# A message-passing layer on one core: relative destinations read from one SBUF partition, in place of memory, and whole loads in place of queued parts

## The chip, the cores and the metric

The kernel runs on one core of one Trainium2 chip. Its time is device microseconds of one execution; the number given for a kernel is the median over its runs. Engines are named as in the profile: PE (TensorE), DVE (VectorE), ACT (ScalarE), POOL (GpSimd) and SP (SyncE, which here only issues DMAs). SBUF is the on-chip memory with 128 partitions, HBM the large memory outside.

## The reference

A graph has 6250 nodes with 128 features each and 100000 edges, sorted by destination. For every edge the features of its source node, of its destination node and of the edge itself go through one linear layer, a layer norm and a ReLU. The messages are summed by source node, added to the nodes, and layer-normed again.

```python
def _L0_gnn_ref(x, edge_index, edge_attr, W, b, gamma, beta):
    row, col = (edge_index[0], edge_index[1])          # src, dst
    msg_in = jnp.concatenate([x[row], x[col], edge_attr], axis=-1)
    h = msg_in @ W + b
    mu = jnp.mean(h, axis=-1, keepdims=True)
    var = jnp.mean(jnp.square(h - mu), axis=-1, keepdims=True)
    h = (h - mu) * jax.lax.rsqrt(var + LN_EPS) * gamma + beta
    msg = jax.nn.relu(h)
    return jax.ops.segment_sum(msg, row, num_segments=x.shape[0])

x = _layernorm(x + _L0_gnn_ref(x, stack([src, dst]), edge_attr_128, ...), axis=-1)
```

## The kernel before, in words

The edges are cut into 782 tiles of 128 edges. Four tiles make a piece; there are 196 pieces, and the main loop runs one piece per slot. Piece numbers are q in the code. Five splits of the tiles (164, 168, 168, 164 and 118) are handled one after another: while the pieces of one split go through the first stage, the pairs of node blocks of the split before go through the second.

First stage, for a piece q. `edge_loads` (L471) brings in eT, the transposed edge features (128 features x 1024 edges, float32, two pieces), and db (128 partitions x 1024, bfloat16), which holds in every partition the same row: for each of the 1024 edges the destination relative to the first destination of its piece. `edge_window` (L506) loads win, the 42 rows of the projected node table that the piece's destinations lie in, three bfloat16 parts one above the other (126 partitions). `edge_hot` (L518) compares db with the partition's number on DVE (L528) and so makes the one-hot matrix ohd. `edges` (L531) multiplies on PE: eT with its part of the weights (L540) and ohd with win (L544), both into the PSUM tile hp. `scatters` (L548) copies hp to one of eight hs buffers on ACT (L552, L553), and POOL writes each tile's 128 rows with an indirect DMA (L557) to their places in the table `sorted` in HBM, where the edges of a block of source nodes lie together. Pieces 0 and 1 (`BY_PE = 2`) don't use db: PE repeats their row.

Second stage, for a pair of node blocks: `load_pair` (L600, DMA at L604) brings its rows of `sorted` back as hl (four buffers), and the class `Pair` adds the source node's projection, norms, applies the ReLU and sums by node, over PE, ACT and DVE. `clear` (L191) fills the unused places of `sorted` from an SBUF tile of 48 partitions that holds empty rows. The last split's pairs form the tail, with no first stage beside them.

Where the relative destinations come from: `windows` (L264) computes on DVE the tile drel, 98 partitions x 2 x 512, bfloat16. One partition holds the rows of two pieces, 2 KB. When its second half is done, POOL stores drel to the HBM tensor drel_d (L271), and every db load reads its row of drel_d 128 times (step 0 over the partitions of db).

The loads of eT and db: up to q = 8 (`FROM = 9`) one DMA each for two pieces (for q = 0 one for each piece), and for piece 2 db's load is on POOL's queue. From q = 10 on `edge_loads` issues nothing itself; it appends six parts to the list `parts`: four DMAs of eT with 32 partitions each, and after the second and the fourth of them one DMA of db with 64 partitions. `part_loads` (L502, DMA at L504) issues the next one on SP. It is called three times a slot: before `edge_hot`, before `scatters`, and at the slot's end, so that the six parts go out over two slots.

The order of PE, DVE, ACT and SP is written out by hand (`manual_schedule`): each engine does its instructions in the order in which the code issues them. A slot q of the main loop (L901 to L931) calls in this order: steps of the node projections (first split), `edge_loads` and `edge_window` up to four pieces ahead, `clear_pairs`, `part_loads(1)`, `edge_hot(q + 2)`, `edges(q)`, one step of `work` (the second stage, which also issues the hl loads), `part_loads(1)`, `scatters(q)`, steps of `places`, the rest of `work`, `part_loads(1)`. SP waits in this order too: a DMA whose buffer is not free holds up those behind it. eT and db have three buffers of two pieces each, win six.

Of the kernel before, what the change touches and what calls it, by code (L numbers as in the profile page):

```python
# [9 lines left out]
BF16 = mybir.dt.bfloat16  # L10
# [6 lines left out]
P = 128  # L17
# [5 lines left out]
TILES = 782  # L23
# [4 lines left out]
PT = 4  # L28
# [3 lines left out]
PIECES = 196  # L32
TABLE_FROM = [0, 13, 45, PIECES]
HALF = PIECES // 2
# [31 lines left out]
def dram_ap(t, offset, ap):  # L66
    return bass.AP(tensor=t.tensor, offset=t.offset + offset, ap=ap)
# [12 lines left out]
def flat(t):  # L80
    return t.rearrange("p t d -> p (t d)")


def fast_path(ctx, tc, io, bad_d):
# [3 lines left out]
    nc = tc.nc  # L88
    first_tile = first_tiles()
    const = ctx.enter_context(tc.tile_pool(name="const", bufs=1))  # L90
    dram = ctx.enter_context(tc.tile_pool(name="dram", bufs=1, space=bass.MemoryType.DRAM))
    psum = ctx.enter_context(tc.tile_pool(name="psum", bufs=1, space=bass.MemoryType.PSUM))

    xb_d = [dram.tile([3, hi - lo, D], BF16, name=f"xb_d{k}") for k, (lo, hi) in enumerate(TABLES)]
    drel_d = dram.tile([PIECES, PT * P], BF16, name="drel_d")
    sorted_d = [dram.tile([NB * k * P + n * P, ROW], F32, name=f"sorted{s}")
                for s, (n, k, _, _) in enumerate(SPLITS)]

# [5 lines left out]
    setup = early.enter_context(tc.tile_pool(name="setup", bufs=1))  # L104
# [154 lines left out]
    nc.vector.memset(ones_f, 1.0)  # L259
    dst_f = setup.tile([HALF, 2, PT * P], F32, name="dst_f")  # L260

    drel = setup.tile([HALF, 2, PT * P], BF16, name="drel")

    def windows(k):  # L264
        if k == 0:
            nc.vector.tensor_copy(flat(dst_f), flat(dst_i))
        else:
            nc.vector.tensor_scalar(drel[:, k - 1, :], dst_f[:, k - 1, :], dst_f[:, k - 1, 0:1],
                                    None, op0=ALU.subtract)
        if k == 2:  # L270
            nc.gpsimd.dma_start(drel_d.rearrange("(p h) e -> p (h e)", h=2), flat(drel))  # L271

    def check_windows():
        ends = setup.tile([HALF, 2, 2], F32, name="ends")
# [193 lines left out]
        nc.gpsimd.memset(h[:, :, D:ROW], 0.0)  # L468
    held = {}

    def edge_loads(q, queue=None):  # L471

        if q % DG or q >= PIECES:
            return
        t0 = q * PT
        g = min(DG, PIECES - q)
        eT = edge.tile([P, DG * PT * P], F32, name="eT", bufs=3)
        db = edge.tile([P, DG * PT * P], BF16, name="db", bufs=3)
        for n in ([(0, g)] if q else [(i, 1) for i in range(g)]):
            c0, c1 = n[0] * PT * P, min((n[0] + n[1]) * PT * P, (TILES - t0) * P)  # L480
            if q > FROM:
                continue
            nc.sync.dma_start(eT[:, c0:c1], io["eT"][:, t0 * P + c0:t0 * P + c1])
            c1 = (n[0] + n[1]) * PT * P
            if q + n[0] < BY_PE:
                continue
            (nc.sync if q > 2 else nc.gpsimd).dma_start(
                db[:, c0:c1], dram_ap(drel_d, t0 * P + c0, [[0, P], [1, c1 - c0]]))
        held[q // DG] = (eT, db)
        if q > FROM:  # L490
            e1 = min(g * PT * P, (TILES - t0) * P)
            for i in range(4):
                a = slice(i * 32, (i + 1) * 32)
                parts.append((eT[a, :e1], io["eT"][a, t0 * P:t0 * P + e1]))
                if i % 2:
                    parts.append((db[(i - 1) * 32:(i + 1) * 32, :g * PT * P],
                                  dram_ap(drel_d, t0 * P, [[0, 2 * 32], [1, g * PT * P]])))

    FROM = 9
    parts = []  # L500

    def part_loads(n):  # L502
        for _ in range(min(n, len(parts))):
            nc.sync.dma_start(*parts.pop(0))  # L504

    def edge_window(q):  # L506
        if q >= PIECES:
            return
        k = sum(q >= x for x in TABLE_FROM[1:])
        base = nc.values_load(base_c[0:1, q:q + 1], engines=[mybir.EngineType.SP],  # L510
                              min_val=0, max_val=TABLES[k][1] - TABLES[k][0] - WN,
                              skip_runtime_bounds_check_because="kept inside the table")
        win = edge.tile([P, D], BF16, name="win", bufs=6)
        i = nc.sync.dma_start(win[:3 * WN, :], xb_d[k][:, bass.ds(base, WN), :])  # L514
        held["win", q] = win
        return i

    def edge_hot(q):  # L518
        if q >= PIECES:
            return  # L520
        m = min(PT, TILES - q * PT)
        c0 = q % DG * PT * P
        db = held[q // DG][1][:, c0:c0 + m * P]
        if q < BY_PE:
            db = psum.tile([P, PT * P], F32, name="sel", bufs=BANKS["sel"])
            nc.tensor.matmul(db, ones_h[0:1, :], drel[0:1, q, :], start=True, stop=True)
        oh = edge.tile([P, PT * P], BF16, name="ohd", bufs=3)
        nc.vector.tensor_scalar(oh[:, :m * P], db, part_w, None, op0=ALU.is_equal)  # L528
        held["oh", q] = oh

    def edges(s, q):  # L531
        t0 = q * PT
        m = min(PT, TILES - t0)
        c0 = q % DG * PT * P
        eT = held[q // DG][0][:, c0:c0 + m * P]
        oh, win = held.pop(("oh", q)), held.pop(("win", q))
        hp = psum.tile([P, PT, P], F32, name="hp", bufs=2)
        for j in range(m):
            at = slice(j * P, (j + 1) * P)
            nc.tensor.matmul(hp[:, j, :], eT[:, at], w[:, 2, :], start=j == 0, stop=False,  # L540
                             skip_group_check=True)
        for j in range(m):
            at = slice(j * P, (j + 1) * P)
            nc.tensor.matmul(hp[:, j, :], oh[:3 * WN, at], win[:3 * WN, :],  # L544
                             start=False, stop=j == m - 1, skip_group_check=True)
        held["hp", q] = hp
# [222 lines left out]
    def run(g, n=1):  # L769
        for _ in range(n):  # L770
            next(g, None)
# [22 lines left out]
    load_x(1, 1)  # L794
    load_x(2, 1)
    windows(0)
    run(groups[0], 2)
    windows(1)
    windows(2)
    run(groups[0], 3)  # L800
    edge_loads(0)
    edge_loads(2)
    run(first)
    bases([0])
# [54 lines left out]
    def work(n):  # L859

        nonlocal n_steps
        for _ in range(n):
            for off, step in FLOW:
                i = n_steps - LEAD - off
                if i % 4 or not 0 <= i // 4 < len(pairs):
                    continue
                if step is None:
                    load_pair(*pairs[i // 4])
                    continue
                if off == 0:  # L870
                    at_work[i // 4] = Pair(*pairs[i // 4])
                step(at_work[i // 4])
            n_steps += 1
# [7 lines left out]
    def steps_due(q):  # L881
        for (q0, n0), (q1, n1) in zip(due, due[1:]):
            if q0 <= q < q1:
                return n0 + (n1 - n0) * (q - q0) // (q1 - q0)
        return 0
# [3 lines left out]
    def clear_pairs(s, n):  # L889
        for p0 in range(cleared[s], min(cleared[s] + n, NB // 2)):  # L890
            i = clear(s, p0, 1, nc.sync)
            if s == 0:
                tc.declare_no_dep(i.ins, group="early", reason="see check_early")
                tc.add_to_no_dep_group("clear", i.ins)
            cleared[s] = p0 + 1

    ahead = 3
    for s, (n_tiles, _, _, _) in enumerate(SPLITS):
        p0, p1 = first_tile[s] // PT, -(-first_tile[s + 1] // PT)
        slots = p1 - p0  # L900
        for i in range(slots):  # L901
            q = p0 + i
            for g in groups:
                run(g)

            while ahead <= min(q + 4, 3 + q + q // 3):
                edge_loads(ahead)
                edge_window(ahead)
                ahead += 1
            if s + 1 < n_split and i >= slots - (30 if s else 26):  # L910
                clear_pairs(s + 1, 1 if slots > NB // 2 else 2)
            part_loads(1)
            edge_hot(q + 2)
            edges(s, q)
            n = steps_due(q + 1) - n_steps
            work(min(n, 1))
            part_loads(1)
            scatters(s, q)
            for g in steps_at.pop(q, []):
                run(g)  # L920
            work(n - 1)
            part_loads(1)
            if s == 0:
                if todo and q % 4 != 3:
                    groups = groups[-5:] + [project(*todo.pop(0))]
                    run(groups[-1])
                    if n_todo - len(todo) in loads:
                        load_x(*loads.pop(n_todo - len(todo)))
                clear_pairs(0, 1 + i % 2 if 1 <= i else 0)
            if q in others:  # L930
                others.pop(q)()  # L931
        if s == 0:
            assert not todo and not loads
    s, n = n_split - 1, NB // 2
# [311 lines left out]
```

## Time and profile before

| what | value |
|---|---|
| median of 3 runs | 1183.32 us (1182.11 to 1186.76) |
| the profiled execution | 1186.76 us, its span 1184.8 us |
| mean granted TensorE clock | 0.916 |
| busy: PE, DVE, POOL, ACT | 929.1, 930.7, 839.6, 630.8 us (78, 79, 71, 53%) |
| weight loads on PE | 818.0 us (69%), beside the matmuls |
| SP's DMA queue (q1) | 101908 packets, 189.85 MB, 56.4% of 16 engines |
| POOL's DMA queue (q0) | 25184 packets, 53.31 MB, 13.9% of 16 engines |
| read from and written to HBM | 155.74 MB and 88.11 MB |

The span is the time from the first to the last instruction of the profiled execution. An engine's busy share is a mean over the whole span, in which the first stage (25 to 1040 us) and the tail after it have different limits. A group's line gives the instruction, how often it ran, its busy time and mean duration, and then how long its engine stood idle just before it and what ended most of that. For a DMA queue the profile gives the time that its packets took, as a share of the 16 DMA engines' time. A DMA's line on SP tells how long SP took to issue it; when its data landed is seen only from those that wait for it.

Busy shares in tenths over 40 slices of the span, from the page:

```
PE   3736464448798985989797788978978998899994
DVE  8876566638888895988898778978888866888995
ACT  1323232116554653655565546655564765668995
POOL 2777777777777777777777777777777777614664
DMA  6888887678877875787887578888657776434551
```

### The profile page before, as it was taken

The numbers are of one execution on the slowest core, as the hardware profiler recorded it, in microseconds if no ns is written. First come the engines' busy times: TensorE is split into PE (matmuls) and PEld (weight loads), VectorE is DVE, ScalarE is ACT, GpSimd is POOL, SyncE is SP. The second block draws the span as 40 slices with busy tenths as digits, with TensorE's granted clock in tenths as the row PEclk, the third lists the DMA queues.
The fourth block names the chain that finished last, engine by engine and source line by source line (L and its number), as shares of the span: only waits on it lengthen the run. The fifth ranks groups of instructions, "written<-read, shape, count | busy, mean of one in ns | idle before, by whom it ended". The sixth has DMA issues, their size and how long they took to land.

```text
span 1184.8 us, 27667 instructions
## 1 busy us (share of the span) xinstructions
PE 929.1 (78%) x8918; PEld 818.0 (69%) x8918; DVE 930.7 (79%) x2511; ACT 630.8 (53%) x2854; POOL 839.6 (71%) x899
## 2 busy tenths in 40 slices
PE   3736464448798985989797788978978998899994
PEld 2636464447787874878686777867867887787883
DVE  8876566638888895988898778978888866888995
ACT  1323232116554653655565546655564765668995
POOL 2777777777777777777777777777777777614664
PEclk9977787768998997998999989999998999999997
DMA  6888887678877875787887578888657776434551
GB/s 184 257 240 256 239 247 217 190 204 237 260 220 229 246 215 142 226 250 213 262 235 206 171 222 247 252 235 252 200 155 219 216 213 180 144 100 133 162 166 58
DMA packets 128225, 245.83 MB, mean 207 GB/s; under 512 B 52507, under 2 KB 66348, under 8 KB 128070
## 3 DMA queue, kind: packets, MB, share of 16 engines
q1 hardware_dynamic: 101908, 189.85, 56.4%
q0 software_dynamic: 25184, 53.31, 13.9%
q8 instruction: 73, 1.20, 0.4%
q10 hardware_dynamic: 978, 0.80, 0.2%
q14 instruction: 82, 0.67, 0.2%
HBM read 155.74 MB, written 88.11 MB: 206 GB/s over the span
## 4 chain that ended last, share of the span: by engine, by line
PE 35%; DVE 23%; DMA 18%; SPq 8%; issue 7%; ACT 6%; POOL 2%; ACTq 0%; DVEq 0%; POOLq 0%
DMA db<-drel_d 12%; PE pa L694 9%; PE hp L540 8%; PE sel L653 5%; DVE msg L685 5%; PE sel L649 5%; DVE sc L383 4%; SPq L504 4%; DVE ohe L622 3%; PE beside L420 3%; DVE ohd L528 2%; POOL sorted L557 2%; PE tr L634 2%; SPq L514 2%; ACT sq L670 2%
## 5 line engine op out<-in xcount | busy, mean ns | idle before, releaser
L557 POOL DMA_INDIRECT sorted<-hs,place_i x782 | 772.2, 988 | 251.0 <-issue 201.6
L670 ACT ACTIVATE sq<-sel 128x128 f32<-128x128 f32 x875 | 230.2, 280 | 107.7 <-DVE sel L663 88.0
L552 ACT COPY hs<-hp 128x512 f32<-128x512 f32 x196 | 114.2, 583 | 289.1 <-PE hp L544 176.4
L694 PE MATMUL pa<-msg,ohe 128*128 128x130 f32 x1900 | 251.7, 287 | 15.4 <-DVE acc L702 14.2
L540 PE MATMUL hp<-w,eT 128*128 128x128 f32 x1564 | 237.6, 300 | 22.0 <-DMA db<-drel_d 9.1
L685 DVE SCALAR_TENSOR_TENSOR msg<-sel,rstd,cut 128x128 f32<-128x128 f32 x875 | 247.1, 345 | 8.7
L694 PEld LDWEIGHTS pa<-msg,ohe 128*128 128x128 f32 x1900 | 233.0, 199 | 17.6 <-issue 8.0
L653 PEld LDWEIGHTS <-ohn 128*128 128x128 bf16 x2850 | 181.0, 100 | 87.2 <-issue 73.5
L540 PEld LDWEIGHTS hp<-w,eT 128*128 128x128 f32 x1564 | 213.0, 211 | 24.2 <-issue 16.7
L528 DVE TENSOR_SCALAR ohd<-db,part_w 128x512 bf16<-128x512 bf16 x194 | 72.7, 375 | 185.0 <-DMA db<-drel_d 132.3
L653 PE MATMUL sel<-xa,ohn 128*128 128x128 bf16 x2625 | 187.2, 223 | 6.9 <-DVE msg L685 3.3
L670 ACT ACTIVATION_READ_ACCUMULATOR sq<-sel 128x1 f32 x875 | 184.3, 211 | 0.0
L649 PE MATMUL sel<-hl,ident 128*128 128x512 f32 (+1 forms) x250 | 131.2, 607 | 48.2 <-DVE msg L685 45.8
L622 DVE TENSOR_TENSOR ohe<-hl,beside 128x1024 f32<-128x1024 f32 (+1 forms) x125 | 144.3, 1155 | 14.0 <-PE pa L694 9.5
L638 ACT COPY ohn<-tr 128x1024 bf16<-128x1024 bf16 (+1 forms) x125 | 120.6, 964 | 26.7 <-PE tr L634 24.8
L634 PE MATMUL tr<-ident_h,ohe 128*128 128x128 bf16 x950 | 75.4, 222 | 18.1 <-DVE ohe L622 9.5
L544 PE MATMUL hp<-win,ohd 126*128 126x128 bf16 x782 | 80.5, 228 | 8.7 <-DVE ohd L528 7.4
L673 ACT ACTIVATE std<-ss,eps 128x4 f32<-128x4 f32 (+1 forms) x250 | 74.3, 297 | 8.1
L649 PEld LDWEIGHTS sel<-hl,ident 128*128 128x128 f32 x250 | 38.3, 193 | 52.8 <-DVE msg L685 50.1
L634 PEld LDWEIGHTS <-ohe 128*128 128x128 bf16 x950 | 59.0, 100 | 21.8 <-DVE ohe L622 13.0
L544 PEld LDWEIGHTS <-ohd 126*128 126x128 bf16 x782 | 64.5, 103 | 12.9 <-DVE ohd L528 8.1
L663 DVE TENSOR_TENSOR sel<-sel,hl 128x512 f32<-128x512 f32 x100 | 69.0, 690 | 5.1 <-PE sel L653 5.1
(157 smaller groups left out, 920.6 us busy)
## 6 DMA issues: line engine op xcount, KB each, us to landing
hl<-sorted SPq DMA_DIRECT2D x100, 528.0 KB
eT<-in_eT SPq DMA_DIRECT2D x368, 128.0 KB
sorted<-empty SPq DMA_DIRECT2D x125, 198.0 KB
db<-drel_d SPq DMA_DIRECT2D x186, 128.0 KB
sorted<-hs,place_i POOLq DMA_INDIRECT x782
hl<-sorted SPq DMA_DIRECT2D x25, 396.0 KB
win<-xb_d SPq DMA_DIRECT2D x196, 31.5 KB
xb_d<-xb SPq DMA_DIRECT2D x16, 384.0 KB
```

What stands on the lines that cost most here:

```text
L540: nc.tensor.matmul(hp[:, j, :], eT[:, at], w[:, 2, :], start=j == 0, stop=False, skip_group_check=True)
L544: nc.tensor.matmul(hp[:, j, :], oh[:3 * WN, at], win[:3 * WN, :], start=False, stop=j == m - 1, skip_group_check=True)
L552: evict = nc.scalar.copy(hs[:, :m, 0:D], hp[:, :m, :])
L557: i = nc.gpsimd.indirect_dma_start(out=sorted_d[s][:, :], out_offset=bass.IndirectOffsetOnAxis(ap=place_i[:parts, t:t + 1], axis=0), in_=h ...
L622: nc.vector.tensor_tensor(self.ohe[:, :k, :], self.hl[:, :k, D:D + 1].to_broadcast([P, k, P]), row_bc(iota_p, k), op=ALU.is_equal)
L634: nc.tensor.transpose(tr[:, j, :], half[:, j0 + j, 1::2], ident_h)
L638: nc.scalar.copy(self.ohn[:, :self.k, :], self.tr[:, :self.k, :])
L649: nc.tensor.matmul(sel[:, :m, :], ident, rows, start=True, stop=False)
L653: nc.tensor.matmul(sel[:, j, :], self.ohn[:, j0 + j, :], xa[:, b, i * D:(i + 1) * D], start=not on_pe and i == 0, stop=(j == m - 1 and i = ...
L670: nc.scalar.activation(sq[:, j, :], self.sel[g][:, j, :], AF.Square, accum_out=ss[:, j:j + 1])
L685: nc.vector.scalar_tensor_tensor(self.msg[:, j0 + j, 0:D], self.sel[g][:, j, :], rstd[:, j:j + 1], cut, op0=ALU.mult, op1=ALU.max)
L694: nc.tensor.matmul(self.pa[:, h, :], self.ohe[:, j, :], self.msg[:, j, :], start=(j == h), stop=(j == k - 2 + h))
```

## The change

The tile drel moves from the pool `setup`, which is given back after the first split, to `const`. It is no longer stored to HBM; the tensor drel_d is gone. A db load now has as its source one partition of drel, number q // 2, with step 0 over the 128 partitions of db: the same 2 KB row, 128 times, from SBUF to SBUF. The parts are gone: for every even q `edge_loads` issues one DMA for eT (128 partitions x 1024) and one for db, at once, on SP, as before for q up to 8. For piece 2 db's load stays on POOL's queue.

```diff
-    drel_d = dram.tile([PIECES, PT * P], BF16, name="drel_d")
...
-    drel = setup.tile([HALF, 2, PT * P], BF16, name="drel")
+    drel = const.tile([HALF, 2, PT * P], BF16, name="drel")
...
-        if k == 2:
-            nc.gpsimd.dma_start(drel_d.rearrange("(p h) e -> p (h e)", h=2), flat(drel))
...
+    def rel_row(k, c0, c1):
+
+        row = flat(drel)[k:k + 1, c0:c1]
+        return bass.AP(tensor=row.tensor, offset=row.offset,
+                       ap=[list(row.ap[0]), [0, P], [1, c1 - c0]])
+
     def edge_loads(q, queue=None):
...
         for n in ([(0, g)] if q else [(i, 1) for i in range(g)]):
             c0, c1 = n[0] * PT * P, min((n[0] + n[1]) * PT * P, (TILES - t0) * P)
-            if q > FROM:
-                continue
             nc.sync.dma_start(eT[:, c0:c1], io["eT"][:, t0 * P + c0:t0 * P + c1])
             c1 = (n[0] + n[1]) * PT * P
             if q + n[0] < BY_PE:
                 continue
             (nc.sync if q > 2 else nc.gpsimd).dma_start(
-                db[:, c0:c1], dram_ap(drel_d, t0 * P + c0, [[0, P], [1, c1 - c0]]))
+                db[:, c0:c1], rel_row(q // 2, c0, c1))
         held[q // DG] = (eT, db)
-        if q > FROM:
-            e1 = min(g * PT * P, (TILES - t0) * P)
-            for i in range(4):
-                a = slice(i * 32, (i + 1) * 32)
-                parts.append((eT[a, :e1], io["eT"][a, t0 * P:t0 * P + e1]))
-                if i % 2:
-                    parts.append((db[(i - 1) * 32:(i + 1) * 32, :g * PT * P],
-                                  dram_ap(drel_d, t0 * P, [[0, 2 * 32], [1, g * PT * P]])))
-
-    FROM = 9
-    parts = []
-
-    def part_loads(n):
-        for _ in range(min(n, len(parts))):
-            nc.sync.dma_start(*parts.pop(0))
...
-            part_loads(1)
             edge_hot(q + 2)
             edges(s, q)
             n = steps_due(q + 1) - n_steps
             work(min(n, 1))
-            part_loads(1)
             scatters(s, q)
...
             work(n - 1)
-            part_loads(1)
```

## The prediction

> **What bounds the kernel now.** I read the page's groups by line first, then the scatters on GpSimd in order of time, then the DVE line that builds the one-hots, then the chain of waits, then the DMA queues of a steady stretch. The page's groups:
>
> ```profile
> L557 POOL DMA_INDIRECT sorted<-hs,place_i x782 | 772.2, 988 | 251.0 <-issue 201.6
> L528 DVE TENSOR_SCALAR ohd<-db,part_w 128x512 bf16<-128x512 bf16 x194 | 72.7, 375 | 185.0 <-DMA db<-drel_d 132.3
> ```
>
> POOL is idle before its scatters for 251.0 us, but 201.6 of that is "issue": the 0.30 us between one scatter and the next. The order of time on POOL shows how regular they are:
>
> ```profile
> 991.16 0.96 POOL L557 DMA_INDIRECT sorted<-hs,place_i  x1 [0.30 <-issue]
> 992.43 0.97 POOL L557 DMA_INDIRECT sorted<-hs,place_i  x1 [0.30 <-issue]
> 993.70 0.97 POOL L557 DMA_INDIRECT sorted<-hs,place_i  x1 [0.30 <-issue]
> ```
>
> One each 1.27 us, so the eight of two slots (a "pair": one eT tile, one db tile) cost 10.2 us. The DVE line has its first and last start in the view of the tile db:
>
> ```profile
> L528 DVE TENSOR_SCALAR ohd<-db,part_w x194: 281/352/583, 24.8 to 1025.5; 128x512 bf16<-128x512 bf16 x193, 128x256 bf16<-128x256 bf16 x1
> ```
>
> (1025.5 - 24.8) / 193 x 2 = 10.37 us a pair. So from 25 to 1040 us POOL sets the pace. The chain nevertheless gives 12% to the loads of db:
>
> ```profile
> DMA db<-drel_d 12%; PE pa L694 9%; PE hp L540 8%; PE sel L653 5%; DVE msg L685 5%; PE sel L649 5%; DVE sc L383 4%; SPq L504 4%; DVE ohe L622 3%; PE beside L420 3%; DVE ohd L528 2%; POOL sorted L557 2%; PE tr L634 2%; SPq L514 2%; ACT sq L670 2%
> ```
>
> and its pieces show why: the last part of a db tile is issued on SP behind an hl load that waits for PE, and lands 4.6 us later, just when DVE wants it.
>
> ```profile
> 934.76 0.35 SPq L604
> ...
> 935.15 4.58 DMA db<-drel_d
> ...
> 939.83 0.35 DVE ohd L528
> ```
>
> These waits and POOL's pitch run side by side: hs has eight buffers, so POOL has scatters in hand while DVE waits. Taking the waits away can at most close POOL's real gaps: 1040.3 - 25.0 = 1015 us between first and last scatter, less 782 x 1.27 = 993, is 22 us.
>
> The DMA queues from 400 to 600 us, where the rows are share of 16 engines' time:
>
> ```profile
> q1 hardware_dynamic: 16490, 33.28, 58.6%
> q0 software_dynamic: 5000, 10.60, 16.8%
> ```
>
> Per pair an engine works 0.586 x 10.37 = 6.1 us for SP's queue and 0.168 x 10.37 = 1.7 us for the scatters; 2.5 us are left. In the trace's records of single packets more than 17 are in flight in 3.3% of the span only, so each of the 16 engines handles about one packet at a time: a slow packet holds its engine.
>
> **The change, part by part.** Removed: the store of drel on POOL (0.78 us, at 13.0) and the wait of 3.46 us before the first db load there (17.24). POOL's next work is the first scatter, which waits for ACT until 24.95 whatever POOL did before; I take 0, bounds 0 and -4 us. Moved: eT and db are no longer queued in parts (four eT, two db) over two slots, at points where SP has just waited for an hl load, but as one eT and one db load at the head of the even slot, ahead of that slot's win and hl loads. SP issues 962 DMAs instead of 1334. At 0.4 to 0.5 us each SP saves some 160 us, none of it on the path. The eT load still waits for PE to be done with the tile three pairs back, so db is issued some two slots (10.4 us) before DVE needs it, instead of 4.6. Behind that wait now stand db, two win loads and an hl load. win is asked for four slots ahead and hl about two and a half, so a wait of a few us there has cover. The eT packets (4,096 bytes) took 214 ns on average in the quarters and 209 in the few whole loads before 50 us: no gain taken, at best 8 x 55 ns = 0.4 us of an engine a pair.
>
> Changed, and the term that decides: the source of db. Before, 128 rows of 2,048 bytes came out of HBM; these packets took 84 ns (median), 108 ns on average, so 8 x 108 ns = 0.86 us of each engine a pair. Now all 128 rows come out of one partition of SBUF. No row of the trace has that. The nearest is the clear, sorted<-empty: its source is 48 partitions, three for each engine. From 60 to 242 us its 1,968 packets of 4,224 bytes took 164 ns in the quick half, but 32% took 300 ns or more, mean 265; the scatters of the same stretch, packets of the same size from 128 partitions to HBM, took 190 on average and only 5% were over 300. So engines that read from few partitions get into each other's way, at two and three times the quick duration. The lower bound is no such effect: 8 x 84 ns = 0.67 us. The upper is that one partition delivers to all engines together what it delivers to one: 4,224 bytes in 164 ns are 25.8 GB/s, and 262,144 bytes take 10.2 us; by the db packets, 128 x 84 ns = 10.75 us. I take 10.5 us for a load. Between ends this far apart the clears decide: 48 partitions already show the effect, and one is further in the same direction.
>
> The Trainium skill, "SBUF — State Buffer", section "Door 1: The DMA port swizzle", has it that DMA bandwidth goes by the SBUF ports that the partitions reach, and that partitions 0 to 3, one port, gave 27.6 GB/s: a load would be 9.5 us by an estimate from that page, and the clears above agree with it in kind. Against it stands "DMA: Bandwidth & Descriptors", section "Where 436 GB/s comes from", whose ceiling for all 16 ports would make the load 0.6 us; by that one the time would be that of the faster rival below.
>
> What 10.5 us of a load does to a pair. If all engines stand in the db load together, the other work of SP's queue comes after it: 6.1 - 0.86 = 5.2 us, in all 15.7 us a pair (the scatters alternate with the db packets on their own queue and can hide). If the engines drift apart, some do their other packets while others read drel, and the pair costs 10.5 us. For the drift: an engine that comes first has the partition to itself and gets through in 0.67 us. Against it: the built program lets each DMA of SP wait for the semaphore of the eighth before it, seven to ten DMAs lie between two db loads for most of the way, so the next db load is often issued only when the last has landed. A second limit is the loop of release, flight and use: eT 8 x 159 ns = 1.3 us, db 10.5, up to 5.2 of others, then two slots of PE (busy 165.8 of 200 us, 8.6 us a pair), over two pairs: 10.2 to 12.8 us. I take half of the 5.2 us as hidden: 13.1 us a pair, 2.73 over 10.37. There are 97 such loads: +265 us. Against the profiled execution, 1186.76 (its span 1184.8 and 2 around it), that is 1452; the median of the runs is 3.4 lower, so 1448 us.
>
> **Rivals.** 1. Lockstep: nothing hidden, 15.7 us a pair: 5.3 x 97 = +517, 1700 us; with 10.75 and the scatters in line too, 17.7 us and 1895. For it: the eight-deep wait. Against it: 2.5 us of idle an engine a pair to give, and the head start that feeds itself. It begins, for me, at 1600. 2. Hidden: the partition is the bottleneck but always busy, 10.2 to 10.75 us beside POOL's 10.2: from 0 to +37 us, 1183 to 1221. For it: the two prices happen to be alike. Against it: it needs every engine's other work out of the way, and no gap between two loads. 3. Faster, one mechanism: the one partition feeds 16 engines at their full rate. Then a load costs 0.67 us, it is issued two slots ahead, the 132.3 us of DVE's waits go, and POOL's gaps close: up to -22 us, 1162. It decides from a db load that lands within the 10.4 us of two slots and leaves the other loads alone, some 3 us. For it: DMA reads of SBUF elsewhere (the scatters) are quick. Against it: the clears. 4. That the change doesn't do what it says, by sending all 128 packets through one engine: 128 x 84 ns = 10.75 us on that engine beside its 5.2 and 1.7: 17.7 us a pair, 1895 too, and counted there.
>
> **How the numbers follow.** Forecast (1230 to 1600) 0.55; lockstep or one engine 0.20; hidden 0.16, of which 0.06 within 0.5% and 0.10 slower; faster 0.09. About 0.5% is what a measurement of this kernel tells from no change, 1177 to 1189. So faster 0.09, same 0.06, slower 0.85. The range from 1190 leaves out 0.15 below, and up to 1800 some 0.05 above.
>
> **What would show it.** Packets of 2,048 bytes near 1 us where they were 0.108, and the share of SP's queue from 56% to far over 70%; if they stay near 0.1 the price is wrong and the kernel is faster. POOL's pitch broken: idle before scatters by ACT hs, beyond the 0.30 us. DVE's wait for db larger, not gone, and hl and win among those waited for. The tail after the last one-hot (1025.5 to the end, 159 us) unchanged; if it grows I missed a term. A pair at 10.4 us with slow packets would mean that they hide.

## The result, and the profile after

| kernel | median, us | lowest to highest | ratio to before (95% interval) |
|---|---|---|---|
| before | 1182.71 (4 runs) | 1182.11 to 1186.76 | |
| changed | 1526.52 (4 runs) | 1522.89 to 1530.11 | 1.2897 (1.2853 to 1.2942) |

The kernel became 344 us slower. The profiled execution took 1530.11 us, its span 1527.8. The groups of the page that answer to those shown of before; POOL's scatters are now L543, the one-hots L514:

```profile
L543 POOL DMA_INDIRECT sorted<-hs,place_i x782 | 765.0, 978 | 610.7 <-ACT hs L539 240.5
L514 DVE TENSOR_SCALAR ohd<-db,part_w 128x512 bf16<-128x512 bf16 x194 | 70.0, 361 | 505.6 <-DMA db<-drel 500.5
```

The instructions themselves are hardly changed (a scatter 978 ns, a one-hot 361 ns). What grew is the idle time before them. POOL's went from 251.0 to 610.7 us: 193.2 us are still "issue", mostly the 0.30 us between scatters, and what ends most of it now is ACT's hs (240.5 us), which itself waits for PE's hp (283.5 us in 116 waits). DVE's wait for db went from 132.3 to 500.5 us. The view of the tile db has its pace:

```profile
L514 DVE TENSOR_SCALAR ohd<-db,part_w x194: 303/352/592, 25.1 to 1370.9; 128x512 bf16<-128x512 bf16 x193, 128x256 bf16<-128x256 bf16 x1
```

(1370.9 - 25.1) / 193 x 2 = 13.95 us a pair, where before had 10.37. Over 97 pairs that is 347 us, the whole of the loss. From the last one-hot to the end it is 157 us, where before had 159. The page's DMA queues over the whole span:

```profile
q1 hardware_dynamic: 95956, 189.83, 74.2%
q0 software_dynamic: 25104, 53.11, 11.3%
```

The same bytes as before (189.85 and 53.31 MB), fewer packets, and yet SP's queue holds the engines for 74.2% of a longer span in place of 56.4%. In the chain that ended last (by engine, then by line), db's loads have 31% where they had 12%, and SP's own instructions (SPq) 21% where they had 8%:

```profile
DMA 37%; PE 26%; SPq 21%; DVE 9%; ACT 4%; issue 3%; ACTq 0%; DVEq 0%
DMA db<-drel 31%; PE pa L680 7%; SPq L194 7%; PE hp L526 5%; PE sel L639 5%; SPq L496 4%; DMA win<-xb_d 4%; PE sel L635 3%; SPq L500 3%; SPq L484 3%; DVE msg L671 2%; PE beside L417 2%; DMA hl<-sorted 2%; PE tr L620 2%; DVE ohe L608 2%
```

A stretch of the chain shows what a db load has become:

```profile
699.40 0.68 SPq L484
...
700.13 12.46 DMA db<-drel
...
712.62 0.35 DVE ohd L514
```

12.46 us from issue to use. Before, the last part of a db tile took 4.58. The reader should also look at how long SP is busy with issuing in this stretch (start, duration, instruction):

```profile
700.13 0.66 SPq L488 DMA_DIRECT2D db<-drel  x1
702.15 6.78 SPq L500 DMA_DIRECT2D win<-xb_d  x2
709.04 1.55 SPq L590 DMA_DIRECT2D hl<-sorted  x1
710.68 1.43 SPq L484 DMA_DIRECT2D eT<-in_eT  x1
712.16 0.56 SPq L488 DMA_DIRECT2D db<-drel  x1
```

The row of 6.78 us covers two win loads and what SP does between them. The loads themselves took 0.80 and 0.77 us; 4.90 us went to the instruction in between, in which SP reads the second win's place in the table, base_c[0, q], from SBUF into a register (TENSOR_LOAD). These reads, changed kernel first:

```profile
L496 SPq TENSOR_LOAD <-base_c x196: 454/780/7809, 26.1 to 1355.7; - x196
L510 SPq TENSOR_LOAD <-base_c x196: 458/707/1862, 17.3 to 1008.1; - x196
```

All of them together took 288 us in the changed kernel and 140 before. So SP is held up behind a slow load not only when it issues DMAs, and here the next db load goes out just as the last one lands.

The cleanest case stands at the start, where piece 2's load is almost alone. It is on POOL's queue, issued at 13.17 us. The queues from 14 to 26 us:

```profile
q0 software_dynamic: 80, 0.26, 68.5%
q1 hardware_dynamic: 790, 0.80, 20.9%
```

0.26 MB on POOL's queue hold 16 engines for 68.5% of 12 us. Beside them SP needs 11.61 us to issue three eT loads that took 2.92 before, PE waits 10.1 us for eT, and the first scatter starts at 32.00 us, not at 24.95.

### The profile page after: what moved, and what is told of

Read it like the earlier page. It is cut to its first block, busy times and chain, and to the rows that moved or that the text cites. A ratio compares the mean times of both kernels' runs of the same rounds, so it can differ in the third digit from the quotient of the medians.

```text
span 1527.8 us, 27117 instructions
## 1 busy us (share of the span) xinstructions
PE 1015.6 (66%) x8918; PEld 878.7 (58%) x8918; DVE 929.3 (61%) x2511; ACT 635.0 (42%) x2854; POOL 831.9 (54%) x898
## 3 DMA queue, kind: packets, MB, share of 16 engines
q1 hardware_dynamic: 95956, 189.83, 74.2%
## 4 chain that ended last, share of the span: by engine, by line
DMA 37%; PE 26%; SPq 21%; DVE 9%; ACT 4%; issue 3%; ACTq 0%; DVEq 0%
DMA db<-drel 31%; PE pa L680 7%; SPq L194 7%; PE hp L526 5%; PE sel L639 5%; SPq L496 4%; DMA win<-xb_d 4%; PE sel L635 3%; SPq L500 3%; SPq L484 3%; DVE msg L671 2%; PE beside L417 2%; DMA hl<-sorted 2%; PE tr L620 2%; DVE ohe L608 2%
## 5 line engine op out<-in xcount | busy, mean ns | idle before, releaser
L543 POOL DMA_INDIRECT sorted<-hs,place_i x782 | 765.0, 978 | 610.7 <-ACT hs L539 240.5
L514 DVE TENSOR_SCALAR ohd<-db,part_w 128x512 bf16<-128x512 bf16 x194 | 70.0, 361 | 505.6 <-DMA db<-drel 500.5
L680 PE MATMUL pa<-msg,ohe 128*128 128x130 f32 x1900 | 262.9, 295 | 39.9 <-DVE acc L688 24.9
L538 ACT COPY hs<-hp 128x512 f32<-128x512 f32 x196 | 114.1, 582 | 400.7 <-PE hp L530 283.5
L680 PEld LDWEIGHTS pa<-msg,ohe 128*128 128x128 f32 x1900 | 243.4, 206 | 44.0 <-issue 35.8
L639 PEld LDWEIGHTS <-ohn 128*128 128x128 bf16 x2850 | 196.6, 106 | 122.5 <-issue 110.0
L526 PE MATMUL hp<-w,eT 128*128 128x128 f32 x1564 | 252.5, 313 | 15.6 <-DMA eT<-in_eT 13.9
L526 PEld LDWEIGHTS hp<-w,eT 128*128 128x128 f32 x1564 | 228.6, 224 | 17.6 <-DMA eT<-in_eT 10.6
L635 PE MATMUL sel<-hl,ident 128*128 128x512 f32 (+1 forms) x250 | 152.4, 696 | 117.8 <-DVE msg L671 117.7
L639 PE MATMUL sel<-xa,ohn 128*128 128x128 bf16 x2625 | 202.1, 234 | 28.1 <-DVE msg L671 27.4
L608 DVE TENSOR_TENSOR ohe<-hl,beside 128x1024 f32<-128x1024 f32 (+1 forms) x125 | 144.4, 1156 | 32.2 <-DMA hl<-sorted 21.3
L530 PE MATMUL hp<-win,ohd 126*128 126x128 bf16 x782 | 84.2, 235 | 91.0 <-DMA win<-xb_d 56.6
L635 PEld LDWEIGHTS sel<-hl,ident 128*128 128x128 f32 x250 | 42.9, 215 | 124.4 <-DVE msg L671 124.2
L417 PE MATMUL beside<-sc,ident_h 128*128 128x294 bf16 (+9 forms) x152 | 27.1, 338 | 69.8 <-DVE sc L402 58.1
```

Of the source, the lines that this page charges most:

```text
L538: evict = nc.scalar.copy(hs[:, :m, 0:D], hp[:, :m, :])
L543: i = nc.gpsimd.indirect_dma_start(out=sorted_d[s][:, :], out_offset=bass.IndirectOffsetOnAxis(ap=place_i[:parts, t:t + 1], axis=0), in_=h ...
L608: nc.vector.tensor_tensor(self.ohe[:, :k, :], self.hl[:, :k, D:D + 1].to_broadcast([P, k, P]), row_bc(iota_p, k), op=ALU.is_equal)
L635: nc.tensor.matmul(sel[:, :m, :], ident, rows, start=True, stop=False)
L639: nc.tensor.matmul(sel[:, j, :], self.ohn[:, j0 + j, :], xa[:, b, i * D:(i + 1) * D], start=not on_pe and i == 0, stop=(j == m - 1 and i = ...
L680: nc.tensor.matmul(self.pa[:, h, :], self.ohe[:, j, :], self.msg[:, j, :], start=(j == h), stop=(j == k - 2 + h))
```

## The experiments

The trace keeps every DMA packet with its size and duration. The table takes db's packets (2,048 bytes; in half_each the 1,024-byte ones) that start between 500 and 900 us. The column of time tells for how much of these 400 us at least one of them was in flight, and the rate is their bytes over that time.

| kernel | median us of runs | packets: mean, half, 90% under (ns) | in flight, us | GB/s |
|---|---|---|---|---|
| before | 1183 | 104, 84, 158 | 135.8 | 74.3 |
| changed | 1527 | 785, 1060, 1118 | 260.4 | 28.7 |
| whole_hbm | 1161 | 92, 84, 85 | 83.9 | 118.7 |
| db_early | 1162 | 105, 84, 151 | 89.1 | 111.8 |
| parts_sbuf | 1580 | 655, 706, 1108 | 262.1 | 28.2 |
| from16_near | 1161 | 144, 84, 311 | 103.2 | 96.5 |
| from16_step4 | 1162 | 95, 84, 131 | 83.3 | 119.6 |
| half_sbuf (half of its loads are from SBUF) | 1290 | 439, 84, 1093 | 208.3 | 45.3 |
| half_each (half of its packets are from SBUF) | 1185 | 131, 46, 485 | 171.7 | 61.1 |
| sbuf_on_act | 1551 | 874, 1067, 1114 | 285.0 | 25.6 |
| sbuf_ahead | 1541 | 881, 1079, 1111 | 281.4 | 26.8 |

**whole_hbm: the change without its source.** db loads read drel_d again; they stay whole and early.

```diff
-                db[:, c0:c1], rel_row(q // 2, c0, c1))
+                db[:, c0:c1], dram_ap(drel_d, t0 * P + c0, [[0, P], [1, c1 - c0]]))
```

> The changed kernel with its db loads reading drel_d in HBM again (and POOL's store back); the loads stay whole and early. Theory A (one source partition is the cost): packets of 2,048 bytes near 0.1 us, POOL's 1.27 us pitch sets the pace again, 1160 to 1190 us. Rival B (the cost is that the loads are no longer queued in parts): still near 1500 us, at least 1300.

Measured: 1160.86 us, 0.9797 of before (0.9773 to 0.982). Theory A holds and rival B falls: the loads in one piece are a gain of 26 us, and the source alone costs the changed kernel 366 us (1526.5 less 1160.9). The page's group of the scatters in this kernel:

```profile
L546 POOL DMA_INDIRECT sorted<-hs,place_i x782 | 768.4, 983 | 244.6 <-issue 202.1
```

POOL is at its pitch throughout: no gap between two of its 782 scatters is over 0.4 us, and from the first to the last they take 1005.6 us (what the line counts beyond "issue" is the wait ahead of the first scatter and more steps of 0.30 us). POOL's scatters and their landings are now what the chain mostly consists of; before, POOL had 2% of it:

```profile
POOL sorted L546 29%; DMA sorted<-hs,place_i 22%; PE pa L683 6%; PE sel L642 4%; ACT sq L659 3%; PE hp L529 2%; PE sel L638 2%; ACT ohn L627 2%; ACT hs L541 2%; ACT fsq L729 2%; PE tr L623 1%; DVE ohe L611 1%; DVE msg L674 1%; ACT std L662 1%; PE beside L420 1%
```

**parts_sbuf: the source alone.** The kernel before, its parts kept, and only the source of db's loads changed (drel lies in const and the store is gone, as in the changed kernel).

```diff
...
-                                  dram_ap(drel_d, t0 * P, [[0, 2 * 32], [1, g * PT * P]])))
+                                  rel_row(q // 2, 0, g * PT * P, 2 * 32)))
```

> The kernel before, its parts kept, but db's parts read from one partition of drel in SBUF. Theory A: the same 256 KB a pair out of one partition, some 9 us a pair beside 5 us of other packets: 1400 to 1600 us. Rival B: 1183 us, like before.

Measured: 1580.35 us, 1.333 of before (1.327 to 1.339). The source is enough for the loss, and its two orders of undoing agree: 366 us with whole loads, 394 us with parts. Cut in halves the packets of one partition still move 28.2 GB/s together.

**from16_near and from16_step4: sixteen partitions in place of one.** The same bytes, packets and destinations, but the source is 16 partitions of drel, each read 8 times.

```diff
-        row = flat(drel)[k:k + 1, c0:c1]
+        row = flat(drel)[0:1, c0:c1]
+        step, _ = row.ap[0]
...
-                       ap=[list(row.ap[0]), [0, P], [1, c1 - c0]])
+                       ap=[[1 * step, 16], [0, P // 16], [1, c1 - c0]])
```

(from16_step4 has 4 * step.)

> The changed kernel with its db loads reading partitions 0 to 15 of drel, each 8 times, so that the one-hots are made of other rows and the output is not the reference's; the bytes and the packets are the same. Theory A, if each partition has a rate of its own: packets near 0.1 us, 1160 to 1200 us. A', if four neighbours share one: packets at 0.3 us, a load 2.3 us, still 1160 to 1230 us. Rival C (SBUF to SBUF is slow whatever the source): packets near 1 us and 1500 us.

> As from16_near, but partitions 0, 4, 8 to 60 (the same part of the output is changed). Each partition with a rate of its own: no difference to from16_near. Four neighbours sharing one: packets at 0.1 to 0.17 us where from16_near has 0.3. Rival C: near 1 us and 1500 us.

Measured: 1161.16 us (0.9794, 0.9768 to 0.9819) and 1161.75 us (0.9799, 0.9772 to 0.9826). Rival C falls: SBUF to SBUF is as quick as HBM to SBUF when the reads are spread. The two differ in their packets only: 16 neighbours have a tenth of their packets over 311 ns, mean 144; with a step of four a tenth is over 131, mean 95. So neighbours seem to share something, though not so that it reaches the time. How many share, these two runs don't settle. Nor does any run tell whether it is the one partition or the same bytes read 128 times that is slow: with sixteen partitions each row is read 8 times only.

The Trainium skill, "SBUF — State Buffer", section "Door 1: The DMA port swizzle", says that four neighbouring partitions share a port and gives 27.6 GB/s for partitions 0 to 3. The 28.7 GB/s here is near that figure, and the difference of the two runs (mean packet 144 and 95 ns) is of the kind that it describes.

**half_sbuf and half_each: half of the bytes, cut in two ways.** In half_sbuf every second db load comes from SBUF. In half_each every load is two: the first half of the row from SBUF, the second from HBM. half_each:

```diff
...
-            (nc.sync if q > 2 else nc.gpsimd).dma_start(
-                db[:, c0:c1], rel_row(q // 2, c0, c1))
+            h0 = (c0 + c1) // 2
+            queue = nc.sync if q > 2 else nc.gpsimd
+            queue.dma_start(db[:, c0:h0], rel_row(q // 2, c0, h0))
+            queue.dma_start(db[:, h0:c1], dram_ap(drel_d, t0 * P + h0, [[0, P], [1, c1 - h0]]))
```

> The changed kernel with every second db load reading drel_d in HBM, the others one partition of SBUF. If what counts is the engines' time added up over both loads (9.0 + 0.9 us for the db packets of two pairs and 2 x 5.2 us for the other packets of SP's queue, 20.3 us) it just fits beside POOL's 20.4 us: 1160 to 1220 us. If each slow load costs its own delay, whatever its neighbour leaves free: the mean of 1527 and 1161, some 1343 us.

> The changed kernel with the first half of every db row from one partition of SBUF and the second half from drel_d in HBM: the same bytes from each as in half_sbuf, but in every pair. At the 29 GB/s that the changed kernel's db packets reached, 4.5 us a pair, beside some 5 us of other packets 9.5 us, under POOL's 10.2: 1160 to 1190 us if it is the burst of 9 us that costs in half_sbuf (1290). If what costs is the bytes out of one partition, however cut: 1290 us again.

Measured: 1290.4 us (1.0917, 1.0886 to 1.0948) and 1185.13 us (1.0017, 0.9995 to 1.0039). half_sbuf fits neither of its two expectations: added-up engine time would have fitted beside POOL, and the mean of both kernels would be 1343. half_each, with the same bytes out of one partition, is 105 us quicker and in the range expected of the burst, though 24 us over whole_hbm. The group of POOL's scatters in both, half_sbuf first:

```profile
L547 POOL DMA_INDIRECT sorted<-hs,place_i x782 | 767.5, 981 | 382.3 <-issue 201.4
```

```profile
L548 POOL DMA_INDIRECT sorted<-hs,place_i x782 | 769.9, 985 | 262.7 <-issue 210.8
```

In half_sbuf POOL stands idle for another 181 us beyond "issue"; the largest part, 121.0 us in 86 waits, is for scatters that have not landed. I read this so: a burst of 9 us delays every queue's transfers at once, and the buffers behind them don't reach that far, while two bursts of 4.5 us nearly hide. The two times are measured; that the buffers are the reason was not tried by itself.

**sbuf_on_act: the slow loads on another queue.**

```diff
-            (nc.sync if q > 2 else nc.gpsimd).dma_start(
+            (nc.scalar if q > 2 else nc.gpsimd).dma_start(
                 db[:, c0:c1], rel_row(q // 2, c0, c1))
```

> The changed kernel with the db loads (one partition of SBUF) issued on ACT's queue instead of SP's. If the other loads are late because they stand behind db's packets in SP's queue, they now alternate with them, some 9 to 10.5 us a pair: 1200 to 1300 us, with packets of 2,048 bytes still near 1 us. If a slow packet holds its engine for all queues alike, or ACT's own waits eat the gain: 1450 us or more.

Measured: 1550.71 us, 1.312 of before (1.305 to 1.319). The second expectation holds. The chain that ended last in this kernel, by line:

```profile
DMA hl<-sorted 24%; DMA db<-drel 9%; PE pa L680 7%; DMA eT<-in_eT 5%; PE hp L526 4%; PE sel L639 3%; PE sel L635 3%; DMA win<-xb_d 3%; SPq L496 2%; SPq L194 2%; DVE ohe L608 2%; PE tr L620 2%; DVE msg L671 1%; DVE sc L380 1%; SPq L500 1%
```

The wait has only changed its name: db's 31% became 9%, and hl, whose packets now alternate with the slow ones, has 24%. The Trainium skill, "DMA: Bandwidth & Descriptors", section "Issuing engines are not separate DMA queues", says that transfers of all queues run on the same 16 engines; this run agrees.

**sbuf_ahead: the slow loads asked for earlier.** db is loaded one pair further ahead, with four buffers, and issued before eT.

```diff
-        db = edge.tile([P, DG * PT * P], BF16, name="db", bufs=3)
+        for k in [q // DG + 1] if q else [0, 1]:
...
+            rows[k] = edge.tile([P, DG * PT * P], BF16, name="db", bufs=4)
+            if k:
+                (nc.sync if k > 1 else nc.gpsimd).dma_start(rows[k], rel_row(k, 0, DG * PT * P))
...
+        db = rows.pop(q // DG)
```

> The changed kernel with db one pair further ahead (four buffers) and issued before eT. If the gaps of some 4.7 us between two db loads come from the next one being asked for too late, engines that are through early can go on to it: 1250 to 1450 us. If SP cannot put it in the queue while the packets of the last one stand there, or the engines are full as it is: 1500 us or more.

Measured: 1541.43 us, 1.3015 of before (1.2958 to 1.3073). The gaps don't come from asking late. The waits of this kernel, longest first:

```profile
ACT hs L539 <- PE hp L531: 376.8, 119, 26.8
DVE ohe L609 <- DMA hl<-sorted: 292.8, 59, 14.9
...
PE hp L527 <- DMA eT<-in_eT: 251.7, 36, 14.5
```

With db early, hl and eT are late instead, so db's place in the order is not what costs. Whether the DMA engines' time or SP's is what runs short, this run doesn't separate: SP's register reads of base_c took 563 us in it.

**db_early: where before lost 26 us.** The kernel before, with db from HBM as one load at the head of the even slot and eT still in four parts.

```diff
         if q > FROM:
+            nc.sync.dma_start(db[:, :g * PT * P],
+                              dram_ap(drel_d, t0 * P, [[0, P], [1, g * PT * P]]))
...
-                if i % 2:
-                    parts.append((db[(i - 1) * 32:(i + 1) * 32, :g * PT * P],
-                                  dram_ap(drel_d, t0 * P, [[0, 2 * 32], [1, g * PT * P]])))
```

> The kernel before, with db from HBM as one load at the head of the even slot; eT stays in four parts. If before lost its 26 us (1187 to 1161) because the last part of db landed just when it was wanted: 1160 to 1170 us. If it lost them by the eT parts (32 partitions, more and smaller DMAs): 1180 to 1187 us.

Measured: 1162.0 us, 0.9835 of before (0.9816 to 0.9854). So most of it (20 us, against 1181.71 for before in the same series) was db's last part, landing just when it was wanted (the run makes db's load whole as well as early and doesn't separate the two). What eT's parts cost beside it is too small for these runs to tell. In the view of the tile db, what ended DVE's idle time before the one-hots:

```profile
  DMA db<-drel_d: 38.0, 18
```

It was 132.3 us in 43 waits.

The version that beats both kernels is whole_hbm, 1160.86 us: the change's loads in one piece, with db's row still read from HBM. Its difference to db_early is not one that these runs can tell.

## Why the prediction was right, and where it was not

What bounds the kernel: right in part. POOL's pitch did set the pace of the scatters for most of the way, but the ceiling of 22 us on what the waits for db were worth had the wrong path, and that whole_hbm came to 1161 us, one microsecond from the 1162 given for closing POOL's gaps, is chance. Of the 22 us only 10 were there to close: from the first scatter to the last it is 1015.3 us before and 1005.6 in whole_hbm, where no gap is left, because not every scatter keeps to 1.27 us. The profiled executions differ by 27.2 us all the same, for the end of the kernel follows the last one-hot (159.3 us from it to the end before, 159.0 in whole_hbm), and that came 26.8 us earlier. 18.5 of these lie in the last 26 one-hots, 163.7 us before and 145.2 in whole_hbm:

```profile
L528 DVE TENSOR_SCALAR ohd<-db,part_w x26: 281/350/560, 861.8 to 1025.5; 128x512 bf16<-128x512 bf16 x25, 128x256 bf16<-128x256 bf16 x1
L517 DVE TENSOR_SCALAR ohd<-db,part_w x26: 330/348/593, 853.5 to 998.7; 128x512 bf16<-128x512 bf16 x25, 128x256 bf16<-128x256 bf16 x1
```

In this stretch DVE waited for db 31.0 us before, in 8 waits, and not once in whole_hbm; db's loads have 26.4% of the chain there, and the rest goes over PE, DVE and ACT with hardly any POOL. The 12% of the chain that the prediction set aside as running beside POOL's pitch were a bound of their own.

The price of a load from one partition: the right mechanism, and 10.5 us was a little high. db's packets were in flight for 260.4 of 400 us, in 3649 / 128 = 28.5 loads: 9.1 us each. The engines together got 28.7 GB/s, 262,144 bytes in 9.1 us; the clear's quick packets had suggested 25.8.

How much of the other packets hides: the step that failed is "I take half of the 5.2 us as hidden". Between two loads' packets there were (400 - 260.4) / 28.5 = 4.9 us in which no db packet was in flight, and 9.1 + 4.9 = 14.0 us is the pair that was measured. The records of single packets from 500 to 900 us tell what hid: of the 4.8 us a pair that an engine spent on the other packets of SP's queue, 1.2 fell into the time of a db load, a quarter and not half, and of the scatters' 1.8 us 0.9. The 3.6 and 0.9 us left over nearly fill the 4.9. That is nearer to the rival of lockstep than to the forecast; the rival's number was 15.7 because the load was priced too high. The two errors have opposite signs (+2.3 us not hidden, of which 0.9 are scatters that were counted as hidden, and -1.4 us on the load). That they nearly cancel is luck. It left the forecast 0.85 us a pair short: 97 x 0.85 = 82 us, 1452 in place of 1534, and the profiled execution took 1530.

Why so little hid is shown in part. The drift was there: from 500 to 900 us a tenth of db's packets took 84 ns and a quarter under 451, so some engines did get through early. But from 600 to 800 us the queues show how little was left over:

```profile
q1 hardware_dynamic: 11443, 24.48, 78.9%
q0 software_dynamic: 3776, 7.98, 13.2%
```

92.1% of 13.95 us are 12.85 us of work for each engine a pair: 8 x 0.785 = 6.3 for db, 4.7 for the rest of SP's queue, 1.8 for the scatters. As before, few packets are in flight beyond one for each engine (more than 17 in 2.0% of the span), so an engine with a slow db packet does little else, and time that I counted as free for other packets was spent waiting. sbuf_on_act and sbuf_ahead, which change queue and order, gained nothing (1551 and 1541 us).

The other reason that the prediction gave for lockstep, the wait of each of SP's DMAs for the eighth before it, can be read from the trace: in the changed kernel that eighth DMA had always landed before SP was through with the instruction ahead, in all 718 cases that can be followed. So this wait cost nothing. Yet db was issued late, on average 1.7 us after the load before had landed (500 to 900 us), and SP itself was held up: from 600 to 900 us its DMA instructions took 227 of 300 us, 21 of them over 3 us each, and its register reads 54 us more; in whole_hbm the DMA instructions took 94 us, none over 3. SP has 21% of the changed kernel's chain and had 8% before, while the prediction put SP's time off the path, with a saving of 160 us. (The profile has 726 DMAs on SP for 1098, not 962 for 1334; the difference is the same.) Asked for a pair earlier, in sbuf_ahead, db gained nothing. How much of the 4.9 us is the engines' and how much SP's, no run separates.

The moved loads: I took 0 for the early, whole loads outside the rival. They are worth -26 us, but only where the source leaves room; in the changed kernel nothing of it is seen. The cover that I named for win and hl was not enough: PE waited 56.6 us for win and DVE 21.3 us for hl.

POOL's store and the wait behind it: I took 0, at best -4 us. The first scatter comes 7.0 us later (32.00 for 24.95). That isn't the store: half_sbuf has the store, its first load on POOL is from one partition too, and its first scatter comes at 32.7. What the term left out is the slow load that now stands there and holds up SP's eT loads. That was in reach: the price of the load was known, and I didn't ask what it would collide with at the start.

What would show it: packets near 1 us (median 1.06), SP's queue from 56.4% to 74.2% (over 70, if not far over), POOL idle by ACT's hs, DVE's wait for db larger, hl and win among what is waited for, the tail unchanged (157 us for 159). All are there.

## What to carry to other kernels

A repeated read costs by where its copies come from: 128 copies of a row from HBM took an engine 0.1 us a packet, the same 128 copies from one SBUF partition 0.8 us, and all queues stood behind them, the issuing engine's own register reads too. Price such a source from the nearest rows whose source is narrow, and count a slow packet as time of its engine that hardly anything else can use, whatever queue it is on. Added-up engine time is still too kind to a burst: the same bytes cost 1290 us as a 9 us load in every second pair and 1185 as a 4.5 us load in every pair. A load that lands just when it is wanted is worth issuing earlier even where another engine seems to set the pace: it gave 2% here, and the chain that ended last had shown it.

## What was not expected of the hardware

SP's issue of a DMA is not a fixed time: before, 95% took under 0.9 us and none over 1.8; behind a slow load single issues took up to 9.9 us (an eT load), without a semaphore being named as what it waited for. SP's read of one number from SBUF into a register went the same way: over 2 us in none of 196 before, up to 7.8 us in the changed kernel. The runs don't tell why.

The packets of one slow load of POOL's queue were 4,096 bytes, two rows each, and took 2.05 us on average, 64 of them; on SP's queue they were 2,048 bytes and 0.79 us.

The granted TensorE clock was lower where PE had less to do: 0.64 from 200 to 400 us with PE busy for 72 of 200 us, against 0.74 from 150 to 260 us before with 59 of 110. The runs don't tell why, and PE bounds neither stretch.
